# A selective scan with its decays in SBUF instead of PSUM, and no pointer for the carried state

## The chip, the cores and the metric

The kernel runs on one core of one Trainium2 chip. The metric is the device time of one launch in microseconds. Everything is float32 except a few small bfloat16 tables.

## The reference, cut to what matters

The input `x` is (4, 512, 64, 64): four images of 512 channels and L = 4096 positions. Two layers follow each other, each with a residual. The first is a group norm, a layer norm over channels, and a Mamba block on four chunks of 128 channels that share weights. The second is a group norm and a linear attention. The change lies in the recurrence of the first:

```python
dt = jax.nn.softplus(jnp.einsum('blr,er->ble', dt, dt_proj_w) + dt_proj_b)
A = -jnp.exp(A_log)
def step(h, inp):
    dt_t, B_t, C_t, x_t = inp
    dA = jnp.exp(dt_t[:, :, None] * A)
    h = dA * h + (dt_t * x_t)[:, :, None] * B_t[:, None, :]
    y = jnp.einsum('bds,bs->bd', h, C_t)
    return (h, y)
```

There are 256 inner channels and 16 states for each image and chunk: 4 x 4 x 256 x 16 recurrences of 4096 positions.

## The kernel before, in words

Time is cut into 8 tiles of T = 512 positions. A step is one image, one time tile and one chunk: N = 128 steps in the order image, tile, chunk. A step has two halves `e` of 128 inner channels. The 128 channels by 16 states of a half are laid out as 4 groups of states `q` by 4 blocks of channels `j`: one tile of 128 partitions holds 32 channels by 4 states. So there are 2 x 4 x 4 scans of 512 positions in a step, 4096 in all. Two scans make a slot, 16 slots a step, and two slots share one tile `h` (4 x 512 columns). "A pair of slots" below is the work of one `h`.

An order written out by hand runs the slots; `slot(g)` issues what belongs to slot g, and `after()` adds a piece of everything else (convolution, projections, norms, attention of the image before) at fixed slots or when a credit of matmul work allows. In a pair of slots:

- `decay` (L713): ScalarE (ACT) computes `dA = exp(dt * A)`, 512 columns, three ahead (`LEAD`), each into a PSUM bank of its own.
- `drive` (L721): GpSimd (POOL) multiplies `u = dt * x` with the row of B, two scans at once, 1024 columns, two slots ahead, into one of three `bx` buffers in SBUF.
- the scan (L739): VectorE (DVE) reads `dA` from PSUM and `bx` from SBUF and writes `h`. Its start value is 0 in the first time tile; later it is a pointer to one column of `st`, the carried states in SBUF.
- POOL copies the last column of `h` to `st` (L750) and multiplies the last quarter of `h`'s columns with the row of C (L751, from `c_sb` in SBUF).
- `product` (L759): DVE multiplies the other three quarters (1536 columns) with `c_all`, which TensorE spreads into a PSUM bank. It is issued after the first scan of the next pair.
- `fold_states` (L761): TensorE folds the states into `y`, a PSUM bank for each half; `take_y` copies it out on ACT, and `gate` (L781) multiplies it on POOL.

`dt` and `u` of a step are made in a tile of two parts (`time_steps`, `to_rows`: L620, L628), go to DRAM as `d_rows` and come back spread over the layout of the scans (`spread`, L639) into `d_all`; the DMAs are queued on SP. The eight PSUM banks are: 1 for `y`, 1 for `c_all`, 3 for `dA`, 3 for all other matmuls (`work_bank`).

Of the kernel before, what the change touches and what calls it, by code (L numbers as in the profile page):

```python
# [24 lines left out]
def kernel(  # L25
# [44 lines left out]
    ps_y = ctx.enter_context(tc.tile_pool(name="ps_y", bufs=1, space=bass.MemoryType.PSUM))  # L70
    ps_c = ctx.enter_context(tc.tile_pool(name="ps_c", bufs=1, space=bass.MemoryType.PSUM))
    ps_d = ctx.enter_context(tc.tile_pool(name="ps_d", bufs=LEAD, space=bass.MemoryType.PSUM))
    ps_w = ctx.enter_context(tc.tile_pool(name="ps_w", bufs=3, space=bass.MemoryType.PSUM))
# [88 lines left out]
    ident = wk.tile([P, P], F32, tag="sq", name="ident", bufs=4)  # L162
# [62 lines left out]
    w_x = wk.tile([P, DI], F32, tag="bx", name="w_x", bufs=3)  # L225
# [37 lines left out]
    a_sb = rows(a_log, wk.tile([P, NH, NST], F32, tag="sq", name="a_sb", bufs=4))  # L263
# [9 lines left out]
    b_qk = wk.tile([P, C], F32, tag="bx", name="b_qk", bufs=3)  # L273
# [15 lines left out]
    a_k = wk.tile([P, NH, KS, NQ], F32, tag="sq", name="a_k", bufs=4)  # L289
# [96 lines left out]
    def mean_of(sums, what, when, stop=True):  # L386

        got = wk.tile([P, T], F32, tag="sq", name=f"got_{what}", bufs=4)

        def take():  # L390
            nc.scalar.copy(got, sums)
            free()

        copied = later(1, take)
        yield
        yield from until(copied)
        yield when
        yield from room(when)
        bank = work_bank(what)
        mm(bank, mean.to_broadcast([P, P]), got, start=True, stop=stop)  # L400
        return bank

    def over_deviation(v, var, name):
        rs = wk.tile([P, T], F32, tag="sq", name=f"rs_{name}", bufs=4)

        def root():
            nc.scalar.activation(rs, var, AF.Ln, bias=eps)
            nc.scalar.activation(var, rs, AF.Exp, scale=-0.5)

        rooted = later(1, root)  # L410
        yield
        yield from until(rooted)
        yield "wide"
        nc.vector.tensor_tensor(v, v, bc(var, NC), ALU.mult)  # L414
        free()
        norming.clear()
        yield

    def layer_norm(v, name):
        while norming:  # L420
            yield "wait"
        norming.append(name)
        yield from room()
        sums = work_bank(f"mu_sums_{name}")
        sums_into(sums, [v[:, c, :] for c in range(NC)], range(NC))
        mu = yield from mean_of(sums, f"mu_{name}", "one ahead")
        yield "wide"
        nc.vector.tensor_tensor(v, v, bc(mu, NC), ALU.subtract)
        free()
        yield "free"  # L430
        sqs = []
        for c in range(NC):
            sqs.append(wk.tile([P, T], F32, tag="sq", name=f"sq_{name}_{c}", bufs=4))
            nc.scalar.activation(sqs[c], v[:, c, :], AF.Square)
            if c == 1:
                yield "free"
        yield from room()
        sums = work_bank(f"var_sums_{name}")
        sums_into(sums, sqs, range(NC))
        var = yield from mean_of(sums, f"var_{name}", "two ahead")  # L440
        yield from over_deviation(v, var, name)
        for c in range(NC):
            nc.scalar.activation(
                v[:, c, :], v[:, c, :], AF.Identity,
                bias=b_sb[:, c : c + 1], scale=g_sb[:, c : c + 1],
            )
            if c % 2:
                yield "free"

    def layer_scale(v, name):  # L450
# [8 lines left out]
        mu = yield from mean_of(sums, f"mu_{name}", None)  # L459
        mu2 = wk.tile([P, T], F32, tag="sq", name=f"mu2_{name}", bufs=4)  # L460
# [8 lines left out]
        sqs = [None] * NC  # L469

        def part(c):
            sqs[c] = wk.tile([P, T], F32, tag="sq", name=f"sq_{name}_{c}", bufs=4)
            nc.scalar.activation(sqs[c], v[:, c, :], AF.Square, bias=about)
# [12 lines left out]
        var = yield from mean_of(sums, f"var_{name}", "two ahead", False)  # L486
# [80 lines left out]
    def shifted_end(f, name):  # L567
        mv = small.tile([P, NC, 2], F32, tag="mv", name=f"mv_{name}", bufs=4)
        for v in range(2):
            nc.vector.tensor_reduce(mv[:, :, v], f[("sum", "square")[v]], AX.X, ALU.add)  # L570
        nc.vector.tensor_scalar(mv, mv, 1.0 / L, None, ALU.mult)
        d2 = small.tile([P, NC], F32, tag="d2", name=f"d2_{name}")
        nc.vector.tensor_tensor(d2, mv[:, :, 0], mv[:, :, 0], ALU.mult)
        nc.vector.tensor_tensor(mv[:, :, 1], mv[:, :, 1], d2, ALU.subtract)
        nc.vector.tensor_tensor(mv[:, :, 0], mv[:, :, 0], f["mv"][:, :, 0], ALU.add)
        return mv
# [41 lines left out]
    def time_steps(f, nm):  # L618
        for e in range(NH):
            nc.scalar.activation(  # L620
                f["both"][:, 0, e, :], f["pt"][e], AF.Softplus, bias=dtb[:, e : e + 1]
            )

    def to_rows(f, v, nm):

        both = f["both"]
        if v:
            nc.gpsimd.tensor_tensor(f["both"][:, 1], f["both"][:, 0], f["xz"][:, 0], ALU.mult)  # L628
        d_rows = dram.tile([P, NH, T], F32, tag=f"d_rows{v}", name=f"d_rows{v}_{nm}")
        f["d_rows", v] = d_rows  # L630
        later(1, lambda: nc.sync.dma_start(d_rows, both[:, v]))

    def spread(f, e, nm):

        d = wk.tile([P, 2, NJ, T], F32, tag="d_all", name=f"d_all_{nm}_{e}")
        for v in range(2):
            src = f["d_rows", v].rearrange("(j i) e t -> i e j t", i=BLK)[:, e]
            for k in range(KS):
                nc.sync.dma_start(d[k * BLK : (k + 1) * BLK, v], src)  # L639
        f["d_all", e] = d  # L640

    def mixers(f, nm):
# [7 lines left out]
        f["both"] = wk.tile([P, 2, NH, T], F32, tag="dt", name=f"dt_{nm}", bufs=1)  # L650
        dtr = f["dtr"] = f["both"][0 : 2 * LANE, 1, NH - 1, :]
# [31 lines left out]
    b_all, c_all, c_sb, dAs, bxs, hs, ys = {}, {}, {}, {}, {}, {}, {}  # L683
# [24 lines left out]
    def decay(k):  # L708
# [3 lines left out]
        dAs[k] = ps_d.tile([P, T], F32, tag="dA", name=f"dA_{k}")  # L712
        nc.scalar.activation(  # L713
            dAs[k], fs[n]["d_all", e][:, 0, j, :], AF.Exp, scale=a_t[:, e, j, q : q + 1]
        )

    def drive(g):

        n, e, q, jj = place(g)
        bxs[g] = wk.tile([P, 2, T], F32, tag="bx", name=f"bx_{g}", bufs=3)  # L720
        nc.gpsimd.tensor_tensor(  # L721
            bxs[g], fs[n]["d_all", e][:, 1, jj * 2 : jj * 2 + 2, :], bc(b_all[g // JJ], 2), ALU.mult
        )

    def slot(g, last, after):
# [4 lines left out]
        if jj == 0:  # L730
            if g + 3 * JJ < last:
                b_row(g + 3 * JJ)
            hs[g // JJ] = wk.tile([P, NJ, T], F32, tag="h", name=f"h_{g}", bufs=2)
        elif g + 1 < last:
            c_tail(g + 1)
        h = hs[g // JJ]
        for i in range(2):
            j = jj * 2 + i
            nc.vector.tensor_tensor_scan(  # L739
                h[:, j, :], dAs.pop(2 * g + i), bxs[g][:, i, :],  # L740
                0.0 if t == 0 else st[:, c, e, q, j : j + 1], ALU.mult, ALU.add,
            )
            if 2 * g + i + LEAD < 2 * last:
                decay(2 * g + i + LEAD)
            if i == 0 and jj == 0 and g:
                product(g - 1)
                fold_states(g - 1, last)
        del bxs[g]
        if jj == JJ - 1:
            nc.gpsimd.tensor_copy(st[:, c, e, q, :], h[:, :, T - 1])  # L750
            nc.gpsimd.tensor_tensor(  # L751
                h[:, :, CUT:], h[:, :, CUT:], bc(c_sb.pop(g // JJ), NJ), ALU.mult
            )
        after()

    def product(g):

        own = hs[g // JJ][:, :, :CUT]
        nc.vector.tensor_tensor(own, own, bc(c_all.pop(g // JJ), NJ), ALU.mult)  # L759

    def fold_states(g, last):  # L761

        n, e, q, _ = place(g)
        if g + 1 < last:
            c_row(g + 1)
# [4 lines left out]
        for j in range(NJ):  # L770
            mm(
                ys[n, e][j * BLK : (j + 1) * BLK, :], fold, h[:, j, :],
# [33 lines left out]
    def attention(b, x1s, stats):  # L806
# [90 lines left out]
        nrm = small.tile([P, NC], F32, tag="nrm", name=f"nrm_{b}")  # L897
# [114 lines left out]
    st = const.tile([P, NC, NH, NQ, NJ], F32, tag="st", name="st")  # L1012

# [65 lines left out]
    for v in range(2):  # L1079
        to_rows(fs[0], v, names[0])  # L1080
    spread(fs[0], 0, names[0])
    for g in range(JJ, 3 * JJ, JJ):
        b_row(g)
    c_row(0)
    for g in range(2):
# [8 lines left out]
    with tc.manual_schedule():  # L1094
        credit, seen, mix, held[0], held_x[0] = 0.0, work["mm"], iter(()), 0, 0
        for n, (b, t, c) in enumerate(steps):
# [10 lines left out]
            for s in range(SLOTS):  # L1107
                def after():
# [5 lines left out]
                    if s == 0 and before is not None:  # L1114
                        take_y(before, n - 1, 1)
                    if s == SLOTS // 2:
                        take_y(f, n, 0)
                    if s < 2:
                        next(last_mix, None)
                    if s == 1:  # L1120
                        spread(f, 1, nm)
                        if before is not None:
                            gate(before, 1)
# [13 lines left out]
                    if s == 4 and nxt is not None:  # L1137
                        to_rows(nxt, 0, names[n + 1])
                        to_rows(nxt, 1, names[n + 1])
# [3 lines left out]
                    if s == 9:  # L1143
                        gate(f, 0)
                        if nxt is not None:
                            spread(nxt, 0, names[n + 1])
# [14 lines left out]
                    limit[0] = 1 if 0 < s < 6 else 2  # L1161
# [14 lines left out]
        fold_states(N * SLOTS - 1, N * SLOTS)  # L1176
# [63 lines left out]
```

## Time and profile before

| | us |
|---|---|
| median of 3 runs | 7943.56 (7939.15 to 7946.87) |
| the profiled execution | 7963.09 |
| its span | 7961.4 |
| PE busy in the span | 6453.6 (81%) |
| DVE | 6977.7 (88%) |
| ACT | 5507.6 (69%) |
| POOL | 6880.5 (86%) |

A group of the profile reads: line, engine and operation, output and inputs, their shapes, the count, then the busy time in us and the mean duration in ns of one, then the idle time of the engine just before, with what ended most of it. A matmul's line is that of the helper `mm`. The span begins with some 120 us of preparation without scans and ends with some 470 us of attention after the last scan.

### The profile page before, as it was taken

What the parts mean: (1) busy time and instruction counts of PE and PEld (TensorE: products, weight loads), DVE (VectorE), ACT (ScalarE), POOL (GpSimd) and SP (SyncE); (2) the same over time, 40 slices, a digit from 0 to 9 for tenths busy, and PEclk for the clock granted to TensorE, in tenths of its full rate; (3) what the DMA queues carried; (4) which work ended last, traced back from release to release, by engine and by line L of the source; (5) the groups of instructions that cost most, each with busy time, mean ns of one, the idle gap of its engine ahead of it and who ended that gap; (6) DMA issues with size and microseconds to landing.
All of it is one profiled execution on the core that took longest, in us unless ns stands there. A gap on an engine that the chain in (4) does not pass through costs nothing.

```text
span 7961.4 us, 90563 instructions
## 1 busy us (share of the span) xinstructions
PE 6453.6 (81%) x24835; PEld 2120.0 (27%) x24880; DVE 6977.7 (88%) x5766; ACT 5507.6 (69%) x8321; POOL 6880.5 (86%) x4597
## 2 busy tenths in 40 slices
PE   5676777677789888888788888898688888888599
PEld 1121212112223222322222223332122332322144
DVE  5999999999999999989999999998999999988600
ACT  4667777777777777767777777677777777777421
POOL 4999999999999899989999899898999999889600
PEclk7888888888899999998899999899899999999799
DMA  5666666666666666777766666677666666676402
GB/s 154 167 168 166 151 155 159 160 155 167 169 179 162 151 163 159 174 189 175 174 155 171 171 157 161 155 185 189 156 167 163 161 161 159 145 194 180 112 32 90
DMA packets 829184, 1265.87 MB, mean 159 GB/s; under 512 B 183912, under 2 KB 317560, under 8 KB 816384
## 3 DMA queue, kind: packets, MB, share of 16 engines
q1 hardware_dynamic: 804736, 1222.32, 61.1%
q0 software_dynamic: 16896, 33.56, 2.4%
q10 hardware_dynamic: 7040, 4.20, 0.2%
q8 instruction: 195, 3.19, 0.2%
q14 instruction: 317, 2.60, 0.1%
HBM read 1052.78 MB, written 206.57 MB: 158 GB/s over the span
## 4 chain that ended last, share of the span: by engine, by line
DVE 33%; PE 21%; ACT 15%; DMA 12%; issue 8%; SPq 6%; POOL 6%; POOLq 0%; ACTq 0%; DVEq 0%
DVE h L739 22%; DVE h L759 9%; DMA d_all<-d_rows 7%; ACT dA L713 5%; PE pq L124 5%; POOL bx L721 4%; PE pc L124 4%; SPq L688 3%; PE y L124 3%; PE pr L124 3%; SPq L639 2%; DMA c_sb<-c_rows 2%; ACT xz L1048 2%; PE po L124 2%; ACT L1048 1%
## 5 line engine op out<-in xcount | busy, mean ns | idle before, releaser
L721 POOL TENSOR_TENSOR bx<-d_all,b_all 128x1024 f32<-128x1024 f32 x2048 | 4824.7, 2367 | 213.3 <-DVE h L739 195.1
L739 DVE TENSOR_TENSOR_SCAN h<-dA,st,bx 128x512 f32<-128x512 f32 x3584 | 4358.9, 1264 | 358.7 <-ACT dA L713 159.0
L713 ACT ACTIVATE dA<-d_all,a_t 128x512 f32<-128x512 f32 x4096 | 2752.9, 687 | 1568.5 <-DVE h L739 1521.8
L759 DVE TENSOR_TENSOR h<-h,c_all 128x1536 f32<-128x1536 f32 x1024 | 1767.5, 1726 | 0.1
L751 POOL TENSOR_TENSOR h<-h,c_sb 128x512 f32<-128x512 f32 x1024 | 1300.2, 1270 | 190.2 <-DMA c_sb<-c_rows 95.2
L124 PE MATMUL y<-h,fold 128*32 128x512 f32 x8192 | 1271.2, 696 | 71.6 <-POOL h L751 67.4
L124 PE MATMUL c_all<-parts,sel 128*128 128x384 bf16 x1024 | 369.9, 361 | 1123.3 <-DVE h L759 1121.7
L124 PE MATMUL pc<-xn,w_cv 128*128 128x512 f32 x2048 | 1045.7, 645 | 122.8 <-DVE xn L414 62.1
L124 PE MATMUL pq<-w_qk,xa 128*128 128x512 f32 x2048 | 965.5, 604 | 7.9 <-issue 5.3
L739 DVE TENSOR_TENSOR_SCAN h<-dA,bx 128x512 f32<-128x512 f32 x512 | 591.2, 1203 | 90.0 <-ACT dA L713 65.1
L124 PEld LDWEIGHTS <-sel 128*128 128x128 bf16 x1280 | 127.1, 99 | 1762.2 <-DVE h L759 1562.5
L124 PEld LDWEIGHTS pc<-xn,w_cv 128*128 128x128 f32 x2048 | 389.5, 201 | 747.1 <-issue 424.7
L124 PEld LDWEIGHTS pq<-w_qk,xa 128*128 128x128 f32 x2048 | 398.6, 196 | 439.6 <-issue 422.4
L124 PE MATMUL pr<-xb,m 128*128 128x512 f32 x1024 | 485.3, 612 | 7.5 <-DMA xb<-x 3.6
L124 PE MATMUL pp<-xn,w_pr 128*128 128x512 f32 x1024 | 477.7, 597 | 4.8 <-DVE xn L414 4.8
L124 PEld LDWEIGHTS y<-h,fold 128*32 128x32 f32 x8192 | 170.6, 114 | 644.0 <-issue 344.9
L124 PE MATMUL y<-xz,dg 32*32 32x512 f32 x2048 | 337.3, 734 | 0.0
L781 POOL TENSOR_TENSOR xz<-xz 128x512 f32<-128x512 f32 x256 | 325.7, 1272 | 9.2 <-ACT xz L778 9.2
L832 ACT ACTIVATE kq<-pq 128x512 f32<-128x512 f32 x256 | 150.5, 588 | 259.9 <-PE pq L124 259.2
L124 PE MATMUL pd<-xz,w_xp 128*128 128x512 f32 x512 | 323.4, 764 | 7.8 <-ACT xz L1048 7.8
L628 POOL TENSOR_TENSOR dt<-dt,xz 128x1024 f32<-128x1024 f32 x128 | 302.3, 2361 | 24.7 <-ACT dt L620 24.6
L124 PE MATMUL pz<-xn,w_z 128*128 128x512 f32 x512 | 275.4, 631 | 11.7 <-ACT xz L608 8.2
(179 smaller groups left out, 6034.1 us busy)
## 6 DMA issues: line engine op xcount, KB each, us to landing
d_all<-d_rows SPq DMA_DIRECT2D x2048, 256.0 KB, 6.7
b_all<-b_rows SPq DMA_DIRECT2D x4096, 64.0 KB, 2.2
d_rows<-dt SPq DMA_DIRECT2D x256, 512.0 KB, 3.6
c_sb<-c_rows SPq DMA_DIRECT2D x4096, 16.0 KB, 1.8
xs<-in_x_dram SPq DMA_DIRECT2D x32, 1024.0 KB, 6.3
xn<-in_x_dram SPq DMA_DIRECT2D x32, 1024.0 KB, 6.2
xr<-in_x_dram POOLq DMA_DIRECT2D x32, 1024.0 KB, 10.7
x<-xr SPq DMA_DIRECT2D x32, 1024.0 KB, 4.2
```

What stands on the lines that cost most here:

```text
L124: nc.tensor.matmul(out_, lhsT, rhs, **how)
L628: nc.gpsimd.tensor_tensor(f["both"][:, 1], f["both"][:, 0], f["xz"][:, 0], ALU.mult)
L639: nc.sync.dma_start(d[k * BLK : (k + 1) * BLK, v], src)
L688: nc.sync.dma_start(dst[k * BLK : (k + 1) * BLK, :], rows_[q * KS + k, :].partition_broadcast(BLK))
L713: nc.scalar.activation(dAs[k], fs[n]["d_all", e][:, 0, j, :], AF.Exp, scale=a_t[:, e, j, q : q + 1])
L721: nc.gpsimd.tensor_tensor(bxs[g], fs[n]["d_all", e][:, 1, jj * 2 : jj * 2 + 2, :], bc(b_all[g // JJ], 2), ALU.mult)
L739: nc.vector.tensor_tensor_scan(h[:, j, :], dAs.pop(2 * g + i), bxs[g][:, i, :], 0.0 if t == 0 else st[:, c, e, q, j : j + 1], ALU.mult, AL ...
L751: nc.gpsimd.tensor_tensor(h[:, :, CUT:], h[:, :, CUT:], bc(c_sb.pop(g // JJ), NJ), ALU.mult)
L759: nc.vector.tensor_tensor(own, own, bc(c_all.pop(g // JJ), NJ), ALU.mult)
L781: nc.gpsimd.tensor_tensor(f["xz"][:, 1, e, :], f["xz"][:, 1, e, :], f["xz"][:, 0, e, :], ALU.mult)
L832: nc.scalar.activation(qk[i], pq, AF.Relu)
L1048: nc.scalar.activation(fs[n]["xz"], fs[n]["xz"], AF.Silu)
```

## The change

`dA` moves from three PSUM banks to three rows of one SBUF tile. Each row has 513 columns; the first is zero and stays so. The three `bx` buffers become a ring of one tile, also 513 columns a row, and the carried state is copied into the first column of `bx`. The scan then runs over 513 columns with start value 0: its first step gives 0 x 0 + state. `h` has a column more, which later readers skip. The copies in are on ACT (`carry_in`), those out on ACT or, in two of a step's eight pairs, on POOL (`carry_out`); they are left out after the last time tile, and `st` is cleared instead.

`u` is now made in place of `dt`, after `dt` has gone out to DRAM, so the two trips to DRAM and back lie at different slots. The freed PSUM banks go to `c_all` (2), `y` (2) and the others (4). The fold of the states comes after the other pieces of its slot, and the spread of the C row is issued at the end of a pair. The squares of the norms use three fixed buffers in place of four rotating ones. `take_y` and `gate` come one slot later.

```diff
-    ps_y = ctx.enter_context(tc.tile_pool(name="ps_y", bufs=1, space=bass.MemoryType.PSUM))
-    ps_c = ctx.enter_context(tc.tile_pool(name="ps_c", bufs=1, space=bass.MemoryType.PSUM))
-    ps_d = ctx.enter_context(tc.tile_pool(name="ps_d", bufs=LEAD, space=bass.MemoryType.PSUM))
-    ps_w = ctx.enter_context(tc.tile_pool(name="ps_w", bufs=3, space=bass.MemoryType.PSUM))
+    ps_y = ctx.enter_context(tc.tile_pool(name="ps_y", bufs=2, space=bass.MemoryType.PSUM))
+    ps_c = ctx.enter_context(tc.tile_pool(name="ps_c", bufs=2, space=bass.MemoryType.PSUM))
+    ps_w = ctx.enter_context(tc.tile_pool(name="ps_w", bufs=4, space=bass.MemoryType.PSUM))
...
+        sqs = [sqb[:, i, :] for i in (1, 2, 0, 1)]
+        for c in range(2):
             nc.scalar.activation(sqs[c], v[:, c, :], AF.Square)
-            if c == 1:
-                yield "free"
+        yield "free"
         yield from room()
         sums = work_bank(f"var_sums_{name}")
-        sums_into(sums, sqs, range(NC))
-        var = yield from mean_of(sums, f"var_{name}", "two ahead")
+        sums_into(sums, sqs, (0, 1))
+        for c in range(2, NC):
+            nc.scalar.activation(sqs[c], v[:, c, :], AF.Square)
+        yield "free"
+        sums_into(sums, sqs, (2, 3))
...
     def to_rows(f, v, nm):
 
-        both = f["both"]
-        if v:
-            nc.gpsimd.tensor_tensor(f["both"][:, 1], f["both"][:, 0], f["xz"][:, 0], ALU.mult)
         d_rows = dram.tile([P, NH, T], F32, tag=f"d_rows{v}", name=f"d_rows{v}_{nm}")
         f["d_rows", v] = d_rows
-        later(1, lambda: nc.sync.dma_start(d_rows, both[:, v]))
+        nc.sync.dma_start(d_rows, f["dt"])
+
+    def times_input(f):
+        nc.gpsimd.tensor_tensor(f["dt"], f["dt"], f["xz"][:, 0], ALU.mult)
...
+    RING, ROW = 3, T + 1
+    bx = const.tile([P, RING, 2, ROW], F32, tag="bx", name="bx")
+    dA = const.tile([P, LEAD, ROW], F32, tag="dA", name="dA")
...
-        dAs[k] = ps_d.tile([P, T], F32, tag="dA", name=f"dA_{k}")
+        dAs[k] = dA[:, k % LEAD, :]
         nc.scalar.activation(
-            dAs[k], fs[n]["d_all", e][:, 0, j, :], AF.Exp, scale=a_t[:, e, j, q : q + 1]
+            dAs[k][:, 1:], fs[n]["d_all", e][:, 0, j, :], AF.Exp, scale=a_t[:, e, j, q : q + 1]
         )
...
+    def carry_in(g):
+
+        n, e, q, _ = place(g)
+        got = st[:, steps[n][2], e, q, :].rearrange("p (r i) -> p r i", r=JJ)
+        r = g % RING
+        if r + JJ <= RING:
+            nc.scalar.copy(bx[:, r : r + JJ, :, 0], got)
+        else:
+            for k in range(JJ):
+                nc.scalar.copy(bx[:, (r + k) % RING, :, 0], got[:, k, :])
+
+    def carry_out(g, copy):
+
+        n, e, q, _ = place(g)
+        b, t, c = steps[n]
+        if t < NT - 1:
+            copy(st[:, c, e, q, :], hs[g // JJ][:, :, T])
...
+        pooled = g % SLOTS in (AWAY[0], AWAY[1] + 1)
         for i in range(2):
             j = jj * 2 + i
             nc.vector.tensor_tensor_scan(
-                h[:, j, :], dAs.pop(2 * g + i), bxs[g][:, i, :],
-                0.0 if t == 0 else st[:, c, e, q, j : j + 1], ALU.mult, ALU.add,
+                h[:, j, :], dAs.pop(2 * g + i), bx[:, g % RING, i, :], 0.0, ALU.mult, ALU.add,
             )
+            if i == 1 and jj == JJ - 1 and not pooled:
+                carry_out(g, nc.scalar.copy)
             if 2 * g + i + LEAD < 2 * last:
                 decay(2 * g + i + LEAD)
+            if i == 0 and jj == JJ - 1 and g + 1 < last:
+                carry_in(g + 1)
             if i == 0 and jj == 0 and g:
                 product(g - 1)
-                fold_states(g - 1, last)
-        del bxs[g]
         if jj == JJ - 1:
-            nc.gpsimd.tensor_copy(st[:, c, e, q, :], h[:, :, T - 1])
+            if pooled:
+                carry_out(g, nc.gpsimd.tensor_copy)
+            if t == NT - 1 and g % SLOTS == SLOTS - 1:
+                nc.gpsimd.memset(st[:, c], 0.0)
...
+            if g + 1 < last:
+                c_row(g + 1)
         after()
+        if jj == 0 and g:
+            fold_states(g - 1)
...
-                    if s == 4 and nxt is not None:
-                        to_rows(nxt, 0, names[n + 1])
-                        to_rows(nxt, 1, names[n + 1])
+                    if s in (4, 8) and nxt is not None:
+                        to_rows(nxt, int(s == 8), names[n + 1])
+                    if s == 6 and nxt is not None:
+                        times_input(nxt)
+                    if s in (7, 9) and nxt is not None:
+                        spread(nxt, 0, int(s == 9), names[n + 1])
...
-                    limit[0] = 1 if 0 < s < 6 else 2
+                    limit[0] = 2
```

## The prediction

> **What bounds the kernel now.** I read the window table first, split at the first and the last scan: 122 us of preparation, 7372 us in which the 2048 slots run, 468 us of attention after them.
>
> ```profile
> 122.00:7494.00 7372.00, 5968.01 (x23212) 1898.49 (x23240) 6914.12 (x5602) 5370.81 (x8111) 6866.78 (x4579) 0.90 0.67 166
> 7494.00:7962.00 468.00, 427.74 (x1494) 195.76 (x1510) 24.26 (x73) 103.85 (x167) 5.17 (x5) 0.94 0.18 59
> ```
>
> After the length, the columns are PE, PEld, DVE, ACT, POOL, clock, DMA share and GB/s. In the slots DVE is busy 6914 of 7372 us (94%) and POOL 6867 (93%). Both are full, and this only works because they run at the same time. What fills them stands in the page's groups:
>
> ```profile
> L721 POOL TENSOR_TENSOR bx<-d_all,b_all 128x1024 f32<-128x1024 f32 x2048 | 4824.7, 2367 | 213.3 <-DVE h L739 195.1
> L739 DVE TENSOR_TENSOR_SCAN h<-dA,st,bx 128x512 f32<-128x512 f32 x3584 | 4358.9, 1264 | 358.7 <-ACT dA L713 159.0
> L759 DVE TENSOR_TENSOR h<-h,c_all 128x1536 f32<-128x1536 f32 x1024 | 1767.5, 1726 | 0.1
> L751 POOL TENSOR_TENSOR h<-h,c_sb 128x512 f32<-128x512 f32 x1024 | 1300.2, 1270 | 190.2 <-DMA c_sb<-c_rows 95.2
> L739 DVE TENSOR_TENSOR_SCAN h<-dA,bx 128x512 f32<-128x512 f32 x512 | 591.2, 1203 | 90.0 <-ACT dA L713 65.1
> ```
>
> Today every scan has one tensor in SBUF (`bx`) and one in PSUM (`dA`); the large products L759, L414 and L428 also have one of each. POOL reads only SBUF. I therefore looked for the few DVE instructions that have both tensors in SBUF, first by line, then in the timeline (start and duration in us):
>
> ```profile
> L361 DVE TENSOR_TENSOR off_a<-ngm_a,gr_a x4: 161/2306/2314, 56.1 to 4574.4; 128x4 f32<-128x4 f32 x4
> L976 DVE TENSOR_TENSOR m<-m,fold x64: 168/183/2328, 3286.5 to 7845.3; 32x32 f32<-32x32 f32 x64
> L951 DVE TENSOR_TENSOR ob<-pob,bo x16: 128/158/159, 3272.4 to 7844.4; 128x1 f32<-128x1 f32 x16
> ...
> 2003.03 4.56 DVE L739 TENSOR_TENSOR_SCAN h<-dA,bx 128x512 f32<-128x512 f32 x4
> ...
> 2087.02 4.66 POOL L721 TENSOR_TENSOR bx<-d_all,b_all 128x1024 f32<-128x1024 f32 x2
> ...
> 2088.07 1.34 DVE L571 TENSOR_SCALAR mv_b<-mv_b 128x8 f32<-128x8 f32 x1
> ...
> 2089.45 2.26 DVE L573 TENSOR_TENSOR d_b<-mv_b 128x4 f32<-128x4 f32 x1
> ...
> 5835.91 2.33 POOL L721 TENSOR_TENSOR bx<-d_all,b_all 128x1024 f32<-128x1024 f32 x1
> 5835.96 2.30 DVE L361 TENSOR_TENSOR off_b<-ngm_b,gr_b 128x4 f32<-128x4 f32 x1 [1.08 <-POOL gr_b L357]
> 5838.19 1.21 DVE L739 TENSOR_TENSOR_SCAN h<-dA,bx 128x512 f32<-128x512 f32 x1
> ```
>
> The three numbers after a line's count are the shortest, the median and the longest duration in ns. L361 multiplies four columns. It takes 161 ns where POOL is idle, but 2306 where it starts 50 ns after an L721 (5835.91 + 2.33 = 5838.24; 5835.96 + 2.30 = 5838.26): it ends when POOL's product ends. L976 does the same, 183 against 2328. L951, which takes `pob` from PSUM, is never held (128 to 159). So a DVE instruction with two SBUF tensors waits for POOL's product in progress, whatever its own size. A boundary shows who is next: from 2087.02 POOL has two L721 back to back. DVE's L571, whose source and destination are both in SBUF, gets through between them (it ends at 2089.41), and the L573 behind it is held for 2.26 us by the second. The two take turns.
>
> **The change, part by part.** *dA to SBUF.* This gives all 4096 scans two SBUF tensors, beside a POOL that is 93% busy. By the rows above, each scan that finds a POOL product running waits for its end. Whether POOL is held by a running scan no row shows: the two-SBUF instructions of before last at most 0.42 us when free, too short to see it. Between the bounds I take the full exclusion, because the boundary row is a pair taking turns, and a thing that POOL holds whole is most likely held whole by DVE too.
>
> Then the slots last at least POOL's work plus the scans. POOL: 6867 us, less the state copies that go to ACT. Of 1024 copies (204 ns) 224 stay on POOL, so 163 us go, leaving 6704. A scan without pointer has a median of 1197 ns; its 513th element adds 2. A held instruction hides its start under the wait: L361 alone takes 161 ns but ends 20 ns after POOL, so about 138 are hidden, which leaves 1061. Scans that follow a scan cost the pitch instead (1.12: four without pointer span 4.56 in the timeline, (4.56 - 1.20) / 3). Some 3.6 POOL instructions stand against 4 scans in each pair of slots, so I take 1.07. 4096 x 1.07 = 4383. The sum is 6704 + 4383 = 11,087 us in place of 7372. The product L759 (1.73 per pair) has one PSUM tensor and lies beside POOL. Of today's 458 us in which DVE waits in the slots I keep 120, since PE and ACT get half as much again of time for the same work. With 122 + 468 around it: 11,797 by the profiled execution. That one took 7963.09 with a span of 7961.4, 0.25% over the median of 7943.56, so about **11,780**.
>
> The bounds. If POOL is not held, each scan starts where a POOL instruction ends: 6704 / 1024 = 6.55 us of POOL in 3.63 instructions per pair, 1.80 each; four scans take 7.2, the product 1.73 more, 8.9 x 1024 = 9150, with the ends 9740. If nothing of a start is hidden and all of today's waits stay: 6704 + 4096 x 1.199 + 458 + 590 = 12,660.
>
> [...]
>
> *The pointer.* 3584 scans lose 1258 - 1197 = 61 ns (medians): -219 us on DVE, real only if DVE is the bound. Are SBUF reads cheaper in themselves? Two SBUF inputs of 512 took 687 and 690 ns (L285), a PSUM and an SBUF one 678 to 692 (L316): zero. [...]
>
> *ACT.* `dA` to PSUM is 687 ns. SBUF to SBUF with one pointer is 722 (L473) or 710 (L561): +23 to +35, at most 143 us. Carried states: 1024 x 4/3 copies in (a third need two) and 672 out, 2037, at 189 (the 128x1 accumulator read) to 204 ns (POOL's copy): 0.39 to 0.42 ms. ACT goes from 5371 to about 5900. The copy out waits for the scan whose `dA` slot the next decay needs anyway, so the decay behind it is only 0.2 us later, with two scans of slack. In the longer slots all of this is covered; without that cover it is 0.5 ms at most.
>
> *u in dt's place.* POOL's `times_input` now waits for the first `d_rows` to land (issued two slots earlier, 3.6 us to landing, a slot is 3.6) with the next drive behind it. SP's second `d_rows` and spread wait for POOL, with the `b_all` loads three pairs ahead behind them. The spread at slot 9 is needed from slot 14. Priced at nothing; uncovered, 128 x 3.6 = 0.46 ms.
>
> *PSUM, square buffers, fold after the other PE work.* More banks can win at most the scans' 91 us on PE y; the fold moved behind PE pieces can cost as much. The third and fourth square wait on ACT for PE, with decays behind; the same pattern in L473 idles ACT 1.0 us in 128. Nothing, in 11 us pairs.
>
> **The rivals.** *No hold for scans, faster.* A scan takes 1197 ns for 512 elements, over two cycles each at the rate of L759 (1726 for 1536), so it may fetch both tensors without what POOL holds. For: no scan with two SBUF tensors is in the trace. Against: the two-SBUF tensor products wait every time. Then DVE has 6914 - 219 + 8 = 6703, as much as POOL; with today's 458 of waits and 590 around, 7751, near 7730 as a median; less the 91 us on PE y or with ACT's 143 us more, 7640 to 7870. It decides where the scans' mean stays near 1.2 us beside 2.37 us products.
>
> *POOL not held*: slower, about 9740, worked out above; against it the turns at the boundary, for it the missing row.
>
> *ACT becomes the bound*, inside the first rival: its whole 0.5 ms uncovered turns 7750 into 8250. Against: 5900 of 7160 is 82%.
>
> **How the numbers follow.** Full exclusion 0.72, POOL not held 0.08, no hold 0.20 (of which faster 0.17, even 0.01, slower through ACT 0.02). A difference of 0.2% is about what measuring this kernel can tell. Slower is 0.72 + 0.08 + 0.02 = 0.82. The range runs from POOL's bound, 9700, to the upper sum, 12,650; that leaves the no-hold cases and little else out.
>
> **What would show it.** Right: the scans' mean goes from 1.26 to about 2.2 us, because a held instruction counts as busy (10.8 us a pair, less 1.73 and some 0.3 of other DVE work, over four); in the timeline scans end about 1.06 us after a POOL product ends; POOL's products lengthen or idle by about a scan; L759 stays at 1.73, and PE and ACT fall towards half busy. POOL not held: products stay at 2.37 and follow without gaps. Wrong: scans of 1.2 us beside products of 2.37, and a span below 8000.

## The result, and the profile after

The changed kernel takes 11,590.26 us (median of 4 runs, 11,586.39 to 11,593.1) beside 7945.22 for the kernel before (4 runs on the same chip, 7939.15 to 7947.97). The ratio is 1.4589, with an interval of 1.4564 to 1.4614: 3645 us slower. The forecast was 11,780, 1.6% more. The profiled execution took 11,589.92 us with a span of 11,588.2.

The window table of the changed kernel, split again at the first and the last scan (length, PE, PEld, DVE, ACT, POOL, clock, DMA share, GB/s):

```profile
123.00:11121.00 10998.00, 7111.53 (x23188) 2146.64 (x23236) 10732.56 (x5602) 5709.98 (x10147) 8436.07 (x3795) 0.78 0.44 111
11121.00:11588.00 467.00, 429.37 (x1495) 195.57 (x1510) 24.63 (x73) 102.63 (x165) 5.26 (x5) 0.94 0.17 59
```

Everything happened in the slots: 10,998 us in place of 7372, while the attention at the end has 467 in place of 468. DVE has the same 5602 instructions in the slots as before, and its busy time went from 6914 to 10,733 us. The groups of the page say which of them grew:

```profile
L760 DVE TENSOR_TENSOR_SCAN h<-dA,bx 128x513 f32<-128x513 f32 x4096 | 8787.9, 2195 | 294.4 <-issue 82.5
L723 POOL TENSOR_TENSOR bx<-d_all,b_all 128x1024 f32<-128x1024 f32 x2048 | 5675.8, 2771 | 1079.9 <-DVE h L760 1019.8
L716 ACT ACTIVATE dA<-d_all,a_t 128x512 f32<-128x512 f32 x4096 | 2945.7, 721 | 4059.5 <-DVE h L760 3549.1
L776 POOL TENSOR_TENSOR h<-h,c_sb 128x512 f32<-128x512 f32 x1024 | 1708.5, 1668 | 1139.8 <-ACT st L743 788.8
L788 DVE TENSOR_TENSOR h<-h,c_all 128x1536 f32<-128x1536 f32 x1024 | 1763.1, 1722 | 0.1
```

The scans went from means of 1264 ns with a pointer and 1203 without to 2195 ns, POOL's products from 2367 to 2771 and from 1270 to 1668. L788, which takes `c_all` from PSUM, stays at 1722 (1726 before). So of these two groups of DVE only the one whose tensors both lie in SBUF grew. The source view of the scan's line gives shortest, median and longest in ns:

```profile
L760 DVE TENSOR_TENSOR_SCAN h<-dA,bx x4096: 1192/2222/5400, 122.9 to 11119.5; 128x513 f32<-128x513 f32 x196
```

The shortest, 1192, is about that of the scans without pointer before (1184). The work has not become longer; it waits, and the wait counts as busy. The timeline of one plain pair of slots shows for what (start us, duration us; "x2" is two instructions back to back):

```profile
3012.35 1.78 POOL L776 TENSOR_TENSOR h<-h,c_sb 128x512 f32<-128x512 f32 x1 [1.39 <-ACT st L743]
3013.08 1.72 DVE L788 TENSOR_TENSOR h<-h,c_all 128x1536 f32<-128x1536 f32 x1
3014.10 2.35 POOL L723 TENSOR_TENSOR bx<-d_all,b_all 128x1024 f32<-128x1024 f32 x1
3014.73 3.92 DVE L760 TENSOR_TENSOR_SCAN h<-dA,bx 128x513 f32<-128x513 f32 x2
3017.67 3.12 POOL L723 TENSOR_TENSOR bx<-d_all,b_all 128x1024 f32<-128x1024 f32 x1 [1.23 <-DVE h L760]
3018.57 4.42 DVE L760 TENSOR_TENSOR_SCAN h<-dA,bx 128x513 f32<-128x513 f32 x2
3022.18 1.79 POOL L776 TENSOR_TENSOR h<-h,c_sb 128x512 f32<-128x512 f32 x1 [1.39 <-ACT st L743]
3022.91 1.72 DVE L788 TENSOR_TENSOR h<-h,c_all 128x1536 f32<-128x1536 f32 x1
```

Read it as one chain. POOL's L723 ends at 14.10 + 2.35 = 3016.45. Two scans issued at 3014.73 end at 3018.65, so 2.20 us after it. L723 was issued again at 3017.67, in the middle of the second scan; it ends at 3020.79, which is 2.14 after that scan. The next two scans end at 3022.99, 2.20 later, and the L776 issued at 3022.18 ends 0.98 after them. In this pair nothing with two SBUF tensors on DVE advances while a POOL product runs, and no POOL product while such a scan runs; only L788 runs beside POOL. One exchange costs what both cost one after the other, less some 0.1 to 0.3 us of start that is hidden under each wait.

### The profile page after: what moved, and what is told of

The parts are those of the page before. It is cut to its first block, busy times and chain, and to the rows that moved or that the text cites. A ratio compares the mean times of both kernels' runs of the same rounds, so it can differ in the third digit from the quotient of the medians.

```text
span 11588.2 us, 95522 instructions
## 1 busy us (share of the span) xinstructions
PE 7602.5 (66%) x24816; PEld 2368.6 (20%) x24880; DVE 10796.7 (93%) x5768; ACT 5846.8 (50%) x10358; POOL 8448.9 (73%) x3813
## 5 line engine op out<-in xcount | busy, mean ns | idle before, releaser
L760 DVE TENSOR_TENSOR_SCAN h<-dA,bx 128x513 f32<-128x513 f32 x4096 | 8787.9, 2195 | 294.4 <-issue 82.5
L723 POOL TENSOR_TENSOR bx<-d_all,b_all 128x1024 f32<-128x1024 f32 x2048 | 5675.8, 2771 | 1079.9 <-DVE h L760 1019.8
L716 ACT ACTIVATE dA<-d_all,a_t 128x512 f32<-128x512 f32 x4096 | 2945.7, 721 | 4059.5 <-DVE h L760 3549.1
L776 POOL TENSOR_TENSOR h<-h,c_sb 128x512 f32<-128x512 f32 x1024 | 1708.5, 1668 | 1139.8 <-ACT st L743 788.8
L123 PE MATMUL y<-h,fold 128*32 128x512 f32 x8192 | 1431.7, 775 | 1424.3 <-DVE h L788 1422.7
L788 DVE TENSOR_TENSOR h<-h,c_all 128x1536 f32<-128x1536 f32 x1024 | 1763.1, 1722 | 0.1
L123 PE MATMUL pq<-w_qk,xa 128*128 128x512 f32 x2048 | 1141.0, 693 | 10.9 <-issue 6.0
L743 ACT COPY st<-h 128x4 f32<-128x4 f32 x672 | 132.5, 197 | 1196.9 <-DVE h L760 1191.2
L808 POOL TENSOR_TENSOR xz<-xz 128x512 f32<-128x512 f32 x256 | 555.6, 2170 | 3.3 <-ACT xz L805 3.3
L632 POOL TENSOR_TENSOR dt<-dt,xz 128x1024 f32<-128x1024 f32 x128 | 417.4, 3261 | 25.0 <-DMA d_rows<-dt 25.0
L123 PE MATMUL pt<-dt,w_dt 32*128 32x512 f32 x512 | 299.3, 959 | 171.6 <-ACT parts L669 58.9
```

The costliest lines, as they stand in the source:

```text
L123: nc.tensor.matmul(out_, lhsT, rhs, **how)
L632: nc.gpsimd.tensor_tensor(f["dt"], f["dt"], f["xz"][:, 0], ALU.mult)
L716: nc.scalar.activation(dAs[k][:, 1:], fs[n]["d_all", e][:, 0, j, :], AF.Exp, scale=a_t[:, e, j, q : q + 1])
L723: nc.gpsimd.tensor_tensor(bx[:, g % RING, :, 1:], fs[n]["d_all", e][:, 1, jj * 2 : jj * 2 + 2, :], bc(b_all[g // JJ], 2), ALU.mult)
L743: copy(st[:, c, e, q, :], hs[g // JJ][:, :, T])
L760: nc.vector.tensor_tensor_scan(h[:, j, :], dAs.pop(2 * g + i), bx[:, g % RING, i, :], 0.0, ALU.mult, ALU.add,)
```

## The experiments

The theory is that turn-taking: two SBUF tensors on DVE and POOL's reads of SBUF shut each other out, and the whole 3645 us is their time laid end to end. Where the expectations name its rivals by letters, A is that a scan from two SBUF tensors is slow by itself, and C that DVE waits for POOL while POOL isn't held by DVE. D and E came in for what the first run left open: D says that it is the fold behind the other PE pieces, E that it is something else, the way of the carried states through ACT first of all. The times of e2, e3, e4, e6 and e7 are those of one execution each.

**Only the decays back in PSUM (e1_dA_psum).** All of the change stays but the place of `dA`; three banks are found by cutting the others. `dA` and `h` have 512 columns again, a bank for each 128x512 tile of `dA` as in the kernel before, and `limit`, which goes with the number of banks for the other matmuls, has its values of before. Abridged:

```
-    ps_y bufs=2   ps_c bufs=2   ps_w bufs=4
+    ps_y bufs=1   ps_c bufs=1   ps_d bufs=1 (three tags)   ps_w bufs=3
-    dA = const.tile([P, LEAD, ROW], ...)
+    dA = [ps_d.tile([P, T], ..., tag=f"dA{i}") for i in range(LEAD)]
-            if g + 1 < last: c_row(g + 1)
         after()
         if jj == 0 and g:
+            if g < last: c_row(g)
             fold_states(g - 1)
```

> All of the changed kernel but one thing: dA goes back to three PSUM banks, and with it the banks of before (1 for y, 1 for C rows, 3 others); a bank holds 512 columns, so the scan runs over the zero column and 511 positions, and the last position of each time tile is left out. No pointer, carried states through a column of bx, u in dt's place all stay. Theory (two SBUF tensors shut POOL out): the scans are back at about 1.20 us beside POOL products of 2.37, and the time falls from 11,590 to 7640 to 7870 us. Rival A (a scan that reads two SBUF tensors is slow by itself): the same 7640 to 7870, so this run does not tell it apart. Rival B (the copies on ACT, the moved trips to DRAM or the order of the folds cost the 3.6 ms): it stays above 11,000.

Measured: 9143.89 us, ratio 1.1496 (1.1476 to 1.1516). The exclusion is gone, as two rows of its profile show, the scan's by its source view and the product's by the page's groups:

```profile
L761 DVE TENSOR_TENSOR_SCAN h<-dA,bx x4096: 1190/1201/1226, 120.7 to 8667.5; 128x512 f32<-128x512 f32 x196
...
  PE y L124: 950.4, 283
  ACT bx L734: 254.8, 69
  ACT bx L737: 171.4, 73
```

```profile
L724 POOL TENSOR_TENSOR bx<-d_all,b_all 128x1024 f32<-128x1024 f32 x2048 | 4859.5, 2377 | 1366.1 <-DVE h L761 1211.8
```

No scan of 4096 takes more than 1226 ns, and the product is back at 2377. That, with what goes along with it, takes 2446 us off, so B, which would have stayed above 11,000, doesn't hold for the whole. But 1199 over the kernel before remain, where the theory expected none, and they are idle time: the indented lines give, in us and times, what DVE sat waiting for ahead of its scans, 950 us for `y` from PE (91 before) and 426 for the copies into `bx`. The other edits are not free once the exclusion no longer covers them.

**One decay tile of three in SBUF (e2_third).** On top of the last:

```
-    dA = [ps_d.tile(...) for i in range(LEAD)]
+    dA = [(const if i == 0 else ps_d).tile(...) for i in range(LEAD)]
```

> As e1, but one of the three dA tiles lies in SBUF, so every third scan (1365 of 4096) has two SBUF tensors; the last position of each time tile is left out. Theory: POOL's 6704 us plus 1365 x 1.09 = 1488 must follow each other, 8190 in the slots, with the 590 us around them and 100 to 300 of waits 8850 to 9100. Rival A: DVE's 6700 plus 1365 more microseconds of slow scans, about 8100 in the slots and 8800 to 8900 in all; the SBUF scans would take some 2.2 us whether POOL runs or not, and POOL's products would stay at 2.37. Rival B: as e1.

Measured: 9808.74 us, outside the numbers expected, since these had been reckoned without the waits that e1 turned out to have. Against the time measured of e1 it is +665 us for the third of the scans, 0.49 us each, where the whole step from e1 to the changed kernel is 2446 / 4096 = 0.60. DVE's idle time ahead of the scans fell from 1822 us to 1530, so some of the exclusion is absorbed by waits that e1 has anyway. The source view has the two kinds of scan in one line:

```profile
L761 DVE TENSOR_TENSOR_SCAN h<-dA,bx x4096: 1186/1209/5486, 124.7 to 9335.1; 128x512 f32<-128x512 f32 x196
```

Taken apart by the order of issue in the trace, the 1366 scans with `dA` in SBUF have a mean of 1916 ns (1189 to 5486), the other two thirds 1202 and 1205 with none above 1229. So within one kernel the scans that grow are those with two SBUF tensors, and since the shortest of these takes 1189, they aren't slow by themselves: A doesn't fit.

**Half of POOL's product (e3_half_drive).** The changed kernel, with one row of two driven:

```
-            bx[:, g % RING, :, 1:],   d_all[..., jj * 2 : jj * 2 + 2, :], bc(b_all, 2)
+            bx[:, g % RING, 0:1, 1:], d_all[..., jj * 2 : jj * 2 + 1, :], bc(b_all, 1)
```

> The changed kernel, but POOL's product into bx covers one scan of two (512 columns in place of 1024); the other row of bx stays zero, so half of the drive is left out. DVE's instructions are the same. Theory: what POOL does not hold is gained one for one: 2048 x (2.35 - 1.27) = 2210 us less, about 9350 us, with the scans' mean falling from 2.2 to about 1.7. Rival A: DVE is the bound by itself (8790 of scans and 2000 of other work), the time stays above 11,300. Rival B: no change above 5%.

Measured: 9631.82 us, 1958 less than the changed kernel (2210 were expected). The scan's group on its page:

```profile
L760 DVE TENSOR_TENSOR_SCAN h<-dA,bx 128x513 f32<-128x513 f32 x4096 | 6395.3, 1607 | 750.2 <-POOL h L776 180.3
```

The scans are the same instructions on the same tiles, and their mean falls from 2195 to 1607 ns because POOL has less to do. A scan that is slow by itself (A) would have stayed. POOL's products became 1.1 us shorter (median 1277), 2048 of them 2.25 ms, and 1.96 ms of that, 87%, came off the time.

**The two engines by themselves (e4_bench).** A short program of phases, in which DVE and POOL each work through a list with nothing between them:

```
dve:  tensor_tensor_scan(h, a, b, 0.0 or st, mult, add)   # a in SBUF or PSUM, 128x512
pool: tensor_tensor(go, g1, g2, mult)                     # 128x1024; also 128x512, a copy, a memset
```

> The disputed cost by itself: none of the reference is computed. Phases on constant tiles, in this order: scans of 512 with both tensors in SBUF, alone; with one in PSUM, alone; the same with a pointer; both in SBUF with a pointer; POOL products of 1024 alone; then side by side: SBUF scans with POOL products, PSUM scans with POOL products, SBUF scans with POOL products of 512, with POOL copies, with POOL memsets; DVE products with two SBUF tensors, and with one in PSUM, beside POOL products. Theory: a scan alone has the same pitch of about 1.12 us from SBUF as from PSUM; 24 SBUF scans beside 24 products take about 24 x (2.2 + 1.07) = 78 us, 24 products beside 48 PSUM scans 56 us; memsets, which read nothing, hold nothing. Rival A: SBUF scans take over 2 us alone. Rival C (POOL is not held by a running scan): SBUF scans beside products take 56 us, with the products still 2.35 each.

Its timeline, for scans with `a` in SBUF beside products, with `a` in PSUM beside products, and with `a` in SBUF beside memsets:

```profile
177.24 12.77 POOL L42 TENSOR_TENSOR go<-g,g 128x1024 f32<-128x1024 f32 x4 [0.54 <-DVE g L33]
178.14 9.73 DVE L36 TENSOR_TENSOR_SCAN h<-a_s,b 128x512 f32<-128x512 f32 x3
254.87 6.93 POOL L42 TENSOR_TENSOR go<-g,g 128x1024 f32<-128x1024 f32 x3 [0.53 <-DVE g L33]
255.77 4.54 DVE L36 TENSOR_TENSOR_SCAN h<-a_p,b 128x512 f32<-128x512 f32 x4
409.52 4.54 DVE L36 TENSOR_TENSOR_SCAN h<-a_s,b 128x512 f32<-128x512 f32 x4
409.81 3.63 POOL L51 MEMSET go<- 128x1024 f32 x4
```

Divide the duration by the count. With two SBUF tensors both engines run at 3.2 us each (12.77 / 4, 9.73 / 3). With one in PSUM the product takes 6.93 / 3 = 2.31 and the scan 4.54 / 4 = 1.14. Beside a memset, which reads nothing, the SBUF scan takes 1.14 too. The medians of the distance from the end of one instruction to the end of the next, worked out from the trace for each phase:

| DVE | POOL | ns per DVE instruction | ns per POOL instruction |
|---|---|---|---|
| scan, `a` in SBUF | none | 1116 | |
| scan, `a` in PSUM | none | 1114 | |
| scan with pointer, SBUF or PSUM | none | 1175 | |
| none | product of 1024 | | 2298 |
| scan, SBUF | product of 1024 | 3217 | 3216 |
| scan, PSUM | product of 1024 | 1114 | 2299 |
| scan, SBUF | product of 512 | 2137 | 2137 |
| scan, SBUF | copy of 1024 | 1908 | 1908 |
| scan, SBUF | memset of 1024 | 1115 | 894 |
| product of 512, two SBUF tensors | product of 1024 | 2746 | 2746 |
| product of 512, one in PSUM | product of 1024 | 598 | 2306 |

Scan and product alone add to 3414; together they take 3217, and in the trace the ends of the 24 scans and 24 products alternate without an exception. So they take strict turns and hide 0.2 us of their starts. POOL is held as DVE is, which ends C, and the scan from SBUF is as quick as the one from PSUM when left alone, which ends A.

**The fold early again (e5_fold_early).** On top of e1:

```
                 product(g - 1)
+                if g < last: c_row(g)
+                fold_states(g - 1)
...
         after()
-        if jj == 0 and g:
-            if g < last: c_row(g)
-            fold_states(g - 1)
```

> e1 (all of the change with dA in PSUM, the last position of each time tile left out) took 9144 us, 1200 more than the kernel before, with scans of 1.21 us and products of 2.38: DVE waits there 950 us for PE y and 426 for ACT bx. This kernel is e1 with the spread of the C row and the fold put back where they were, before the other pieces of the slot. Theory D (the late fold holds the h buffers back): the 950 go, 8100 to 8300 us are left. Rival E (the copies of the carried state on ACT, with decays and scans behind them, are the cost): stays above 8800, with the waits on ACT grown.

Measured: 8572.69 us, ratio 1.0787 (1.0768 to 1.0807), between the numbers of D and E. What DVE waited for ahead of its scans, by the source view:

```profile
  ACT bx L734: 272.8, 97
  ACT bx L737: 235.5, 100
  ACT st L744: 200.8, 109
...
  PE y L124: 43.9, 36
```

The wait for `y` is gone (950 to 44) and takes 571 us with it, so D has that part. What is left is 709 us of waiting for ACT's copies, into the column (L734, L737) and out of `h` (L744): E has the rest, about 630.

**The fold late, in the kernel before (e6_fold_late).** The reverse, alone:

```
             if i == 0 and jj == 0 and g:
                 product(g - 1)
-                fold_states(g - 1, last)
...
         after()
+        if jj == 0 and g:
+            fold_states(g - 1, last)
```

with what takes `y`, and the gates behind it, a slot later. In the kernel before `fold_states` also issues the spread of the C row, which so moves with it.

> The other side of e5: the kernel before with one thing moved, the fold and the spread of the C row to after the other pieces of the slot (and with them the copies and gates of y one slot later, as in the change). Theory D: 800 to 1100 us slower than before, 8750 to 9050. Rival E: within 100 us of before.

Measured: 8822.76 us, 878 over the kernel before of the same chip (7944.98), where D expected it. The line ahead of its scans in the source view was 90.8, 88 before:

```profile
  PE y L124: 1023.0, 387
```

This edit, which moves no instruction from one engine to another, costs a kernel with full engines 11%. The C row is not what costs: DVE sat idle 0.1 us in all ahead of the product that reads it (L760). Nor is it the later `take_y`: e5 has it too, and waits 44 us for `y`.

**The fold early, in the changed kernel (e7_after_fold_early).** The same edit as in e5, without the C row, on the changed kernel.

> The changed kernel with only the fold put back before the other pieces of its slot; dA stays in SBUF. Theory (scans and POOL products follow each other, and that cover of some 11 us a pair hides everything else): DVE waits only 29 us for PE y there, so no more than 30 to 60 us change, 11,530 to 11,600. Rival (the late fold costs its share in the changed kernel too, and the exclusion is worth only the 2450 us between e1 and it): about 10,500.

Measured: 11,692.51 us, 102 more than the changed kernel and not the little less that was expected. The edit that gives e1 571 us gives this kernel nothing. Its DVE had waited 29 us for `y` in all:

```profile
  PE y L123: 29.4, 21
```

That is the cover at work: with pairs of 10.7 us in place of 7.2, the fold is done in time either way. Why early is 0.9% worse, in one execution, was not pursued.

**The state copies on ACT, in the kernel before (e8_copy_act).**

```
+            if i == 1 and jj == JJ - 1 and t < NT - 1:
+                nc.scalar.copy(st[:, c, e, q, :], h[:, :, T - 1])
-            nc.gpsimd.tensor_copy(st[:, c, e, q, :], h[:, :, T - 1])
```

> The kernel before with one thing of the change that relieves POOL: the copies of the last column of h into st go from POOL to ACT, and are left out in the last time tile. POOL has 209 us less of 6867, ACT 896 x 0.2 = 180 more of 5371. If POOL is a bound in the slots: up to 2% faster, 7780 to 7900. If DVE alone is, or if ACT's copies hold the decays behind them: 7930 to 8050.

Measured: 8013.85 us, ratio 1.0082 (1.0069 to 1.0096). POOL's busy time fell by 186 us (6880 to 6694), and the kernel became 0.8% slower. Less work on POOL is no gain by itself. DVE's waits for `y` and for `dA` rose a little (91 to 124, 224 to 233), by 42 us together, and the wait for `bx` fell by 28. The copy also became something to wait for: POOL sat idle 395 us for it (ACT `st`) ahead of its product with the C row, L752, and the fold's matmuls 197 for that product (67 before). How the 69 us come out of this stays open.

**u in dt's place, in the kernel before (e9_u_in_place).** The tile of `dt`, the product `times_input` and the two round trips through DRAM as in the change, abridged:

```
-                    to_rows(nxt, 0, ...); to_rows(nxt, 1, ...)     # both at slot 4
+                    to_rows at slots 4 and 8, times_input at 6,
+                    spread of the first at 7 and 9, of the second at 0 and 1 of the next step
```

> The kernel before with one part of the change: u is made in dt's place, with the two trips to DRAM and back at the slots of the change. Priced at nothing: 7910 to 7990. If the waits on SP and POOL are not covered: up to 8400 (128 x 3.6 us).

Measured: 7961.38 us, ratio 1.0005 (0.9995 to 1.0015). It costs nothing that can be measured.

**The column filled two slots early (e10_column_early).** On top of e5, which has `dA` in PSUM and the fold early: the copies into the column no longer stand just ahead of their scans in ACT's queue, and all copies out are POOL's, as before the change.

```
-            if i == 0 and jj == JJ - 1 and g + 1 < last:
-                carry_in(g + 1)
...
             drive(g + 2)
+            carry_in(g + 2)        # one copy of two columns per slot
...
-        pooled = g % SLOTS in (AWAY[0], AWAY[1] + 1)
+        pooled = True
```

> e5 (dA in PSUM, no pointer, fold early, the last position of each time tile left out) took 8573 us, with 709 us of DVE waits on ACT's copies of the carried state and 44 on PE y. Here the copies into the column of bx come two slots ahead, one for each slot, and all copies out are on POOL as before. If only the place of the copies in ACT's queue cost, the 709 go and DVE's 219 us of pointers are gained: 7750 to 7950. If 2048 copies on ACT are too many in any place: above 8200.

Measured: 7920.53 us, ratio 0.9955 (0.9939 to 0.9971). E's 630 us are gone, though ACT makes more copies into the column than in the change (2048 of two columns, 382.9 us busy, in place of 1365 with 217). With the copies out ACT spends 383 us on copies here and 350 (217 + 132.5) in the change, yet DVE's wait for the copies into the column is down to 27.5 us and that for ACT's `st` is gone. So it was not their time on ACT but their place in its queue: in the change a copy into the column stands behind a decay that itself waits for a scan, one scan before the value is needed, and the copies out stand in the same queue. What is left is little but the pointer's own worth. The scan's mean fell from 1256 (3584 at 1264 and 512 at 1203) to 1206, by its group in the view of the costliest groups:

```profile
L756 DVE TENSOR_TENSOR_SCAN h<-dA,bx 128x512 f32<-128x512 f32 x4096 | 4744.0, 1206 | 600.4 <-ACT dA L717 289.6 <-PE y L124 153.3 <-POOL bx L724 119.8
```

DVE's scans have 206 us less to do (4358.9 + 591.2 - 4744.0), and their waits for ACT's `dA`, PE's `y` and POOL's `bx` rose from 224, 91 and 78 to 290, 153 and 120 us. With smaller waits that fell, the idle time ahead of the scans rose from 449 to 600 us. That takes back 152 of the 206, and the time falls by about 36 (0.45% of 7954). The PSUM banks are cut here as in e1, so they are not by themselves what e1 lost by. How E's part divides between copies into the column and copies out was not tried apart. Since it leaves out one position of each tile, this kernel shows a price and is no replacement.

## Why the prediction was right

**What bounds the kernel.** Right. DVE and POOL were both full and lived from running at the same time; the change ends that, and the new slots are close to the sum of POOL's work and the scans.

**Full exclusion, chosen between the bounds.** Right, with less support than it needed. The rows of before proved that DVE waits for POOL; that POOL waits for DVE was taken from one boundary where the two alternated, and the instruction that got through there, L571, has one input tensor, so it isn't of the kind in question. To that extent the choice was a good guess. ("At most 0.42 us when free" holds beside POOL only: in the preparation, before the first L721 at 118.6 us, L229 takes 1224 ns with two SBUF inputs and L285 690.) The profile after shows it (2.14 us from the scan's end to the product's, of a product that takes 2.3 alone), and e4 settles it with 3217 and 3216 ns. Beside the memset, the one POOL instruction of e4 that only writes, the scan keeps its pace: 1115 ns, 1116 alone.

**The sum, 1.6% too high.** The slots were to last 11,087 + 120 = 11,207 us and lasted 10,998. Two terms were mis-sized in opposite ways, so part of the nearness is luck. The scan's 1.07 is 1.10 in the pair shown above (2.20 for two): +0.03 x 4096 = +123. POOL's products were put in at full length, though a held product hides its start as a held scan does. In that pair the products that follow a scan end 0.98 and 2.14 us after it, where they have 1.27 and 2.37 when free: 0.29 + 0.23 = 0.52 us, -532 if it held for all 1024 pairs. It doesn't: by the trace 837 of the 1024 L776 and 1065 of the 2048 L723 come straight after a scan. Charge every scan and every POOL instruction of the slots with the time from the last end of either kind to its own: the scans take 4627 us, with the waits ahead of them, where 4383 and 120 of waits were put in (+124); POOL's instructions take 6371 in place of 6704 (-333). Together that is the -209. Last, 11,797 less 0.25% is about 11,770; the 11,780 is ten too high.

**What would show it.** The scans' mean was to be about 2.2 us (2.195), scans were to end about 1.06 us after a product (3.92 long for two from 3014.73, the pair 2.20 after the product's end), POOL's products were to lengthen or idle by about a scan (L723 is 0.40 us longer in the mean and idles 0.53 ahead of each), L759 (L788 after) was to stay at 1.73 (1.72), ACT towards half busy (5847 of 11,588, 50%). PE is at 66%: it was busy 7602.5 us in place of 6453.6, at a granted clock of 0.784 in place of 0.897 over the span; see below.

**ACT's decay, +23 to +35 ns.** 721 ns measured, 687 before: +34. Covered, as said: L716 idles 3549 us for the scans.

**The rivals.** POOL not held (0.08) falls by e4. The price of "no hold for scans", 7640 to 7870, was wrong, though it was not the case that came true: e1 is the run nearest to it (with `dA` in PSUM and the banks of before), and it takes 9144. Three steps under it failed. The fold behind the PE pieces was let cost "as much as 91 us", by the scans' present wait on `y`; that wait is what an early fold leaves over, not what a late one makes, and e6 has 878 us for it. The carried states on ACT were let cost "0.5 ms at most" with 8250 as the end, from ACT's load of 82%; e5 shows about 630, with ACT no bound: DVE waits 709 us there for the short copies in ACT's queue, and 27.5 in e10, where the copies into the column come two slots ahead and those out are POOL's. And the pointer's 219 us were taken off in full: with fold and copies put right, e10 still takes 7921. A faster outcome at 0.17 was therefore too likely: even without the exclusion the rest of this change, as e1 has it, is 15% slower.

**How the parts add.** They don't. With the exclusion in place the fold costs nothing (e7); without it, 571 us (e1 to e5). The whole change costs 3645 us. Taking the exclusion away gives back 2446 of them with the fold late (the changed kernel to e1) and 3120 with the fold early (e7 to e5, with banks and C row as each has them), because the other waits then come out from beneath it. The kernel before with nothing but `dA` in SBUF was not run, so what the exclusion costs by itself is not shown.

**The pointer and u.** The 219 us on DVE are there (206 in e10), and, as the prediction made it a condition, they are real only where DVE is the bound: in e10 about 36 reach the time, for DVE then waits longer for ACT, PE and POOL. `u` in `dt`'s place costs nothing (e9).

## What to carry to other kernels

Before an operand moves from PSUM to SBUF, ask which instructions then read two SBUF tensors on VectorE while GpSimd reads SBUF: in e4 their times were added, 3217 ns for what had been 2299 beside 1114, and this kernel, which lived from both engines running at once, took 10,998 us for slots that had taken 7372. Few such instructions in the trace of before are enough to see half of it, DVE's waiting for POOL, if they are put beside POOL's timeline: a four-column product of 161 ns that takes 2306. The other half took a run. And price every other edit as if the large one were absent: a step that is free in a slow slot (the late fold, 29 us of waiting) was worth 878 us in a fast one.

## What the runs showed of the hardware that was not expected

A scan costs 1114 ns with `a` in PSUM and 1116 with `a` in SBUF, end to end, with its other tensor in SBUF either way (e4); the start value as a pointer adds 60 in either place (1175). That the place of `a` costs nothing the prediction had from L285 and L316, which are no scans, and the pointer's price (61 ns) from scans with `dA` in PSUM alone.

A held instruction on POOL hides part of its start as one on DVE does. In e4 a product ends 2.14 us after the scan before it, in place of 2.30 after another product, and a scan 1.08 after the product, in place of 1.12 after another scan. This is why the pair takes 3217 ns and not 3414.

TensorE's granted clock fell with the longer slots, from 0.90 to 0.78, though PE had the same work and 49% more time for it; the matmuls of the fold took 775 ns in the mean (696 before). e1, e5 and e6 lie between, at 0.86, 0.87 and 0.87 with 9137, 8566 and 8821 us of span. In the changed kernel DVE's scans wait 29 us for PE in all, so there it can have cost little. In e1 and e6 they wait 950 and 1023 us for the fold, and how much of that is the slower clock is not shown; nor is what lowers it.
